# Output projection of a two-layer kernel: tiles transposed once for both of their uses and two tiles later, and one Strassen product moved behind another

## The chip, the core and the metric

The kernel runs on one core of one Trainium2 chip. The metric is the device time of one execution in microseconds (us); the time before is the median of three runs. TensorE is called PE here (PEld is its weight load), VectorE is DVE, ScalarE is ACT, GpSimd is POOL, and SP is the engine whose queue issues nearly all transfers.

## What is computed

A residual stack of two layers on `x` of shape 2 x 1024 x 512. Only the seam between the layers matters here:

```
xn = layernorm(x);  s = attn0(xn) @ Wo;  g = silu(ffn0(xn))
x  = x + s * g                       # the "join": output projection, gate, residual
xn = layernorm(x)                    # 2048 x 512, input of layer 1
s  = linear_recurrence(xn)           # works along time, wants xn with features on partitions
g  = silu(gelu_mlp(xn))              # 512 -> 4096 -> 512, 4-bit weights with scales
x  = x + s * g
```

Layer 1 uses the transposed `xn` twice. The recurrence reads it from DRAM (`xd`, 512 features x 1024 times for each batch); the MLP reads it from SBUF (`xq`), where the features are split into quarters for a Strassen product of 7 instead of 8 block products.

## The kernel before, in words

The rows are cut into 16 tiles of 128, in the order chunk by chunk and within a chunk batch 0, then batch 1 (L154): tile 14 is the last of batch 0 and tile 15 the last of batch 1. All matmuls are fp32; the profile counts two records for each.

**Join (class `Join`, L140).** `product` (L199) adds up 16 matmuls of 128x512 for a tile, one for each head, or 8 where half of the sum was made earlier and lies in DRAM (`pd`: tiles 4, 5, 7, 8, 10, 11, 12, 13). `rest` (L235) is what follows on DVE: add the earlier half (L231), multiply by the gate (L232), add the residual (L224) and write the sum to `x1d` for the end of the kernel (L225), statistics (L219 to L221), a power on POOL (L238) and the normalization (L239), which leaves `xn` in the buffer of the gate, `jg`. `jx` is the buffer of `x`. Products 0 to 2 are made within the last stage of layer 0; `run` (L245) makes products 3 to 15.

**Turn (L277).** For each tile PE transposes `xn` twice, four 128x128 pieces each time: once with the features in their order, for `xd` (ACT copies the PSUM tile into the now free `jx`, one DMA writes it out, L280), and once with even and odd features apart (`step=2`, a strided read), for `xq` (DVE copies, L121). After every second chunk four DVE instructions form the sums of the Strassen quarters (L286 to L289). Tile i is turned right after product i+1. PSUM has three banks for products and two for transposes, and a turn takes both.

**What sets the order.** In `run` the scheduler of the framework orders each engine's instructions at build time, by readiness, so unpacking of the first MLP weights (`hi`, `pk`, `w_g`, `w_u`, `w_d`) is mixed in between on DVE and POOL. In the second layer the order is written out by hand (class `Ordered`, L124). SP's queue is first in, first out: a DMA that waits holds up all behind it. `load_xg` (L188) loads `x` and gate of tile n into one of three buffers (`j_t` has one, `j_t2` two), once the tile three earlier has been turned and written; it is called two tiles ahead. `load_o` (L174) does so for the attention output `jo`, also with three buffers.

**Last tiles.** Tile 14 is turned halfway through product 15 (L260 to L262). Tile 15 is turned in the second layer: `run` returns its `turn`, and `last_turn` (L1582) runs it after five products of the first Strassen group, since that group works on batch 0 alone.

**Second layer.** `four` (L1394) makes the seven products of a weight block: `first` and so on to `seventh`, of two matmuls each, into three PSUM banks a, b, c. The products in bank a accumulate there and ACT takes copies in between; bank c is opened by `third` (P5 of the scheme) and added to by `sixth` (P3), which must wait until DVE has read the bank for `fourth`. The loop at L1594 runs gate (f=0), then up (f=1) for each group and batch. At the very first group and batch (n=0) the order is that of L1610: first, third, second, fifth, fourth, last turn, sixth; the gate's seventh comes in the second slot of the up half.

Of the kernel before, what the change touches and what calls it, by code (L numbers as in the profile page):

```python
# [22 lines left out]
P = 128  # L23
B, T, D = 2, 1024, 512
NT = B * T
KC = D // P
NTT = NT // P
# [36 lines left out]
def done(steps):  # L64
    for _ in steps:
        pass
# [39 lines left out]
def transposed(nc, psp, tag, dst, src, ident, engine, step=1):  # L106


    pt = psp.tile([P, KC, P], F32, tag=tag, name="ptr")
    for j in range(KC):  # L110
        if step == 1:
            s = src[:, j * P : (j + 1) * P]
        else:
            s = src.rearrange("p (kc q par) -> p kc par q", kc=2, par=2)[:, j // 2, j % 2, :]
        nc.tensor.transpose(pt[:, j, :], s, ident)
    if len(dst.shape) == 4:
        pt = pt.rearrange("p (a b) t -> p a b t", b=dst.shape[2])
    if engine == "scalar":
        nc.scalar.copy(dst, pt)
    else:  # L120
        nc.vector.tensor_copy(dst, pt)  # L121


class Ordered:  # L124
# [15 lines left out]
class Join:  # L140
# [47 lines left out]
    def load_xg(self):  # L188
        n = len(self.xg)
        c, b = self.order[n]  # L190
        ti = b * NC + c
        tp = self.tp[n % 3 > 0]
        xt = tp.tile([P, D], F32, tag="x", name=f"jx_{ti}")
        self.tc.nc.sync.dma_start(xt, self.a["x"][ti * P : (ti + 1) * P, :])
        g = tp.tile([P, D], F32, tag="g", name=f"jg_{ti}")
        self.tc.nc.sync.dma_start(g, self.gd[ti * P : (ti + 1) * P, :])
        self.xg.append((xt, g))
# [47 lines left out]
    def run(self, xd, xq, xp):  # L245

        nc, tc = self.tc.nc, self.tc
        with self.ctx as ctx:
            ps_o, ps_t = (
                ctx.enter_context(tc.tile_pool(name=n, bufs=bufs, space=PSUM, reuse_waits="tile"))  # L250
                for n, bufs in (("j_pso", 3), ("j_pst", 2))
            )
            late = None
            for i in range(NTT):
                if i >= self.made:
                    for _ in range(min(i + 3, NTT) - len(self.o)):
                        self.load_o()
                    product = self.product(ps_o, "pso", nc.tensor.matmul)
                    if i == NTT - 1:
                        done(itertools.islice(product, H // 2))  # L260
                        late(nc, ps_t, "pst", self.xg[i - 1][0].rearrange("p (k t) -> p k t", k=KC))
                    done(product)  # L262
                    g = self.xg[i][1]
                    if i == NTT - 1:
                        g = xp.tile([P, D], F32, name="xn_last")
                    for step in self.rest(g):
                        step()
                if late is not None and (i < NTT - 1 or i < self.made - 1):
                    late(nc, ps_t, "pst", self.xg[i - 1][0].rearrange("p (k t) -> p k t", k=KC))
                if late is not None:  # L270
                    for _ in range(min(i + 3, NTT) - len(self.xg)):
                        self.load_xg()
                g = g if i == NTT - 1 else self.xg[i][1]
                late = functools.partial(self.turn, xd, xq, *self.order[i], g)
        return late

    def turn(self, xd, xq, c, b, g, nc, psp, tag, xt):  # L277
        ident = self.cst[:, C_ID, :]
        transposed(nc, psp, tag, xt, g, ident, "scalar")
        nc.sync.dma_start(xd[b].rearrange("k p t -> p k t")[:, :, c * P : (c + 1) * P], xt)  # L280
        h, cols = c % 2, slice(c // 2 * P, (c // 2 + 1) * P)
        quarters = xq[b][:, 0:4].rearrange("p (kc h) par t -> p h kc par t", h=2)[:, h, :, :, cols]
        transposed(nc, psp, tag, quarters, g, ident, "vector", step=2)
        if h:
            b11, b12, b21, b22, t1, t2, t4 = (xq[b][:, q, :, cols] for q in range(7))
            nc.vector.tensor_tensor(t1, b12, b11, ALU.subtract)  # L286
            nc.vector.tensor_tensor(t2, b22, t1, ALU.subtract)
            nc.vector.tensor_tensor(t4, b21, t2, ALU.subtract)
            nc.vector.tensor_tensor(b12, b22, b12, ALU.subtract)  # L289
# [3 lines left out]
def first_layer(ctx, tc, a, cst, minus_half, keep, xnT, od, gd, pd, then):  # L293
# [471 lines left out]
    def within(hg, c, store):  # L765
# [25 lines left out]
        for s in range(NS):  # L791
            turn(pk[:, s, :], k[:, s, :])
# [88 lines left out]
    def finish(hg, c):  # L881
# [42 lines left out]
        for s in range(NS):  # L924
            turn(pot[:, s, :], on[:, s, :])
# [283 lines left out]
def second_layer(ctx, tc, a, cst, x1d, xd, xq, out, late):  # L1209
# [18 lines left out]
    nc = tc.nc  # L1228
# [13 lines left out]
    ident = cst[:, C_ID, :]  # L1242
# [75 lines left out]
    def group_weights(g, w):  # L1318

        g_, u_ = packed("g", g), packed("u", g)  # L1320
        yield
        wg, steps = quartered("g", g, *g_)
        yield from steps
        d_ = packed("d", g)
        wu, steps = quartered("u", g, *u_)
        yield from steps
        wd, steps = halved(g, *d_)
        yield from steps
        w += wg, wu, wd
# [163 lines left out]
    def down(g, b, wd):  # L1493

        left = inters[g, b]
        for i, j, n in (
            (A22, T4, 3), (A11, B11, 0), (A12, B21, 1), (S3, T3, 6), (S1, T1, 4), (S2, T2, 5), (S4, B22, 2)
        ):
            for half in range(2):
                po = ps_o.tile([P, 2, 256], F32, tag="pso", name=f"po_{g}_{b}_{n}_{half}")  # L1500
                for t in range(2):
                    c = (2 * half + t) * P
                    PE.matmul(
                        po[:, t, :], lhsT=left[i][:, c : c + P], rhs=wd[:, j, :], start=True, stop=True
                    )
                dst = acc[b][:, n, half]
                if g == 0:
                    DVE.tensor_copy(dst, po)
                else:
                    DVE.tensor_tensor(dst, dst, po, ALU.add)  # L1510
                yield

    def together(b):


        P1, P2, P3, P4, P5, P6, P7 = range(7)
        for dst, x, y in (
            (P6, P1, P6), (P1, P1, P2), (P7, P6, P7), (P4, P7, P4), (P7, P7, P5), (P5, P6, P5), (P3, P5, P3)
        ):
            for half in range(2):  # L1520
                DVE.tensor_tensor(acc[b][:, dst, half], acc[b][:, x, half], acc[b][:, y, half], ALU.add)
                yield
# [6 lines left out]
    def load_last():  # L1529
        for b, h, i in itertools.islice(ahead, 1):  # L1530
            ti = b * NC + 2 * i + h
            pool, *tags = next(rooms)
            y, x1 = (pool.tile([P, D], F32, tag=t, name=f"l{t}_{ti}") for t in tags)
            nc.sync.dma_start(y, yd[ti * P : (ti + 1) * P, :])
            nc.sync.dma_start(x1, x1d[ti])
            at_last[ti] = y, x1
# [51 lines left out]
    for n in range(2 * NG):  # L1588
        g, b = n // 2, n % 2
        if b == 0:  # L1590
            done(steps)
            wg, wu, wd = weights
            if g < NG - 1:
                weights = []  # L1594
                steps = group_weights(g + 1, weights)
        if n == 2 * NG - 2:
            for _ in range(4):
                load_last()
        if g == NG - 1:
            tog = together(b)  # L1600
        active = n - 1 in starts
        lasts = none
        if n == 2 * NG - 1:
            lasts = down_last(0, wd)
        for f, products in enumerate(up_and_gate(g, b, wg, wu)):
            for s in range(7):
                slot = 7 * f + s
                if n == f == 0:

                    (products[:1] + products[2:3] + products[1:2] + products[4:5] + products[3:4]  # L1610
                     + (last_turn, products[5]))[s]()
                elif s == 1:
                    before()
                else:
                    products[s - (s > 0)]()
                next(downs, None)
                if slot < 10:
                    next(lasts, None)
                if slot not in (0, 2, 4) or not active:
                    next(steps, None)  # L1620
                for _ in range(1 + (slot < 3) if g == NG - 1 else 0):
                    next(tog, None)
                if slot == 7 and n in starts:
                    recurring = recur(*starts[n])
                if slot not in (5, 8, 9):
                    next(recurring, None)
            before = products[6]
        done(downs)
        downs = down(g, b, wd) if g < NG - 1 else none
# [105 lines left out]
```

## Time and profile before

| | us |
|---|---|
| median of 3 runs (3189.05 to 3189.89) | 3189.33 |
| the profiled execution, its own time | 3191.48 |
| its span, first to last instruction | 3188.9 |
| outside the span in that execution | 2.58 |
| PE busy in the span | 3148.8 (99%) |
| DVE / ACT / POOL busy | 2147.2 / 1251.4 / 832.4 |
| join loop, first turn to first product of layer 1 | 1842.59 to 1984.16 |
| layer 1, steady part, PE without a gap | 2010 to 3150 |

How to read it: times in the trace count from the span's start. A timeline row gives start, duration, engine, line, output<-input and, in brackets, the idle time of the engine before it with what ended it. A row "x8" merges eight records. Matmuls are pipelined, so the duration of one record is longer than its share of the engine's time; the distance from the start of one row to the start of the next is what the work took. The granted TensorE clock was 1.00 in every window from 1842.5 to 3150.

### The profile page before, as it was taken

The numbers are of one execution on the slowest core, as the hardware profiler recorded it, in microseconds if no ns is written. First come the engines' busy times: TensorE is split into PE (matmuls) and PEld (weight loads), VectorE is DVE, ScalarE is ACT, GpSimd is POOL, SyncE is SP. The second block draws the span as 40 slices with busy tenths as digits, with TensorE's granted clock in tenths as the row PEclk, the third lists the DMA queues.
The fourth block names the chain that finished last, engine by engine and source line by source line (L and its number), as shares of the span: only waits on it lengthen the run. The fifth ranks groups of instructions, "written<-read, shape, count | busy, mean of one in ns | idle before, by whom it ended". The sixth has DMA issues, their size and how long they took to land.

```text
span 3188.9 us, 38235 instructions
## 1 busy us (share of the span) xinstructions
PE 3148.8 (99%) x12454; PEld 1950.8 (61%) x12454; DVE 2147.2 (67%) x4294; ACT 1251.4 (39%) x2269; POOL 832.4 (26%) x1210
## 2 busy tenths in 40 slices
PE   8999999999999999999999999999999999999998
PEld 6576756666666666666666644555555555555554
DVE  4557678786877878675554454677777666776676
ACT  3466555555555555434333200222222222322223
POOL 2000123222322222222222210332333333333222
PEclk9999999999999999999999999999999999999999
DMA  6244344444444443443334465010001000110014
GB/s 183 64 119 113 112 125 115 115 129 126 119 111 132 135 125 109 111 128 100 87 84 142 117 194 156 30 34 27 27 27 40 27 27 27 34 33 27 27 37 132
DMA packets 499494, 287.40 MB, mean 90 GB/s; under 512 B 207328, under 2 KB 440544, under 8 KB 499296
## 3 DMA queue, kind: packets, MB, share of 16 engines
q1 hardware_dynamic: 490432, 268.97, 29.9%
q0 software_dynamic: 6560, 11.80, 1.3%
q10 hardware_dynamic: 2304, 4.20, 0.4%
q8 instruction: 99, 1.62, 0.2%
q14 instruction: 99, 0.81, 0.1%
HBM read 183.90 MB, written 88.34 MB: 85 GB/s over the span
## 4 chain that ended last, share of the span: by engine, by line
PE 76%; DVE 5%; issue 2%; ACT 1%; DMA 1%; SPq 1%; POOL 0%; DVEq 0%; ACTq 0%; POOLq 0%
PE po L132 15%; PE pua L132 7%; PE pga L132 7%; PE pgate L132 6%; PE pwq L132 5%; PE pwv L132 5%; PE pwk L132 4%; PE zw L132 4%; PE pgc L132 3%; PE puc L132 3%; PE jpo L211 3%; PE pub L132 2%; PE pgb L132 2%; PE pr L132 2%; PE pks L132 1%
## 5 line engine op out<-in xcount | busy, mean ns | idle before, releaser
L132 DVE TENSOR_TENSOR acc<-acc,po 128x512 f32<-128x512 f32 x408 | 277.9, 681 | 208.7 <-PE po L132 207.9
L132 PEld LDWEIGHTS po<-w_d,i 128*128 128x128 f32 x1024 | 194.5, 190 | 142.6 <-issue 111.2
L132 PE MATMUL po<-w_d,i 128*128 128x256 f32 (+1 forms) x1024 | 275.4, 392 | 0.0
L132 PE MATMUL pgate<-xnT,wg 128*128 128x512 f32 x512 | 245.7, 593 | 0.0
L132 PE MATMUL pwq<-xnT,wq 128*128 128x512 f32 x512 | 245.1, 593 | 0.0
L132 PE MATMUL pwv<-xnT,wv 128*128 128x512 f32 x512 | 243.0, 594 | 1.8 <-ACT gate L132 1.8
L132 PE MATMUL pua<-xq,w_u 128*128 128x512 f32 x512 | 240.6, 592 | 0.0
L132 PE MATMUL pga<-xq,w_g 128*128 128x512 f32 x512 | 240.6, 592 | 0.0
L132 PE MATMUL pwk<-xnT,wk 128*128 128x512 f32 x512 | 237.6, 596 | 1.5 <-ACT ka L132 1.5
L132 ACT COPY g<-pga 128x512 f32<-128x512 f32 x96 | 56.2, 585 | 447.2 <-PE pga L132 432.8
L132 DVE SCALAR_TENSOR_TENSOR v<-prewv,cw,v 128x512 f32<-128x512 f32 x192 | 165.9, 865 | 63.4 <-ACT v L132 53.3
L132 PEld LDWEIGHTS po<-w_d,s 128*128 128x128 f32 x720 | 136.8, 190 | 95.4 <-issue 77.0
L132 ACT COPY w<-zw 128x128 f32<-128x128 f32 x192 | 50.6, 264 | 362.0 <-PE zw L132 362.0
L132 DVE TENSOR_TENSOR rr<-rr,zw 128x128 f32<-128x128 f32 x192 | 54.6, 284 | 199.2 <-PE zw L132 195.2
L132 PE MATMUL po<-w_d,s 128*128 128x256 f32 x720 | 184.8, 379 | 0.0
L132 ACT ACT_TABLE_LOAD x133 | 170.6, 1283 | 17.9 <-PE pr L132 11.3
L132 POOL TENSOR_TENSOR rs<-rs,minus_half 128x4 f32<-128x4 f32 x64 | 64.5, 1007 | 429.9 <-DVE rs L132 403.8
L132 POOL TENSOR_TENSOR ot<-ot,gate 128x512 f32<-128x512 f32 x64 | 85.9, 1343 | 343.4 <-ACT ot L132 313.7
L132 DVE SCALAR_TENSOR_TENSOR ka<-prewk,cw,ka 128x512 f32<-128x512 f32 x192 | 150.4, 785 | 34.9 <-ACT ka L132 23.2
L132 PEld LDWEIGHTS zw<-rr,ground 128*128 128x128 f32 x512 | 97.0, 191 | 124.5 <-issue 102.4
L132 DVE SCALAR_TENSOR_TENSOR q<-prewq,cw,q 128x512 f32<-128x512 f32 x192 | 159.8, 833 | 15.0 <-POOL eg L132 6.3
L132 PEld LDWEIGHTS zw<-w,ground 128*128 128x128 f32 x768 | 111.3, 192 | 65.6 <-issue 55.2
(248 smaller groups left out, 6661.6 us busy)
## 6 DMA issues: line engine op xcount, KB each, us to landing
e<-gr SPq DMA_DIRECT2D x64, 256.0 KB, 3.9
de<-e SPq DMA_DIRECT2D x64, 256.0 KB, 3.0
dk<-ka SPq DMA_DIRECT2D x32, 512.0 KB, 2.8
kb<-dk SPq DMA_DIRECT2D x64, 256.0 KB, 3.5
eb<-de SPq DMA_DIRECT2D x64, 256.0 KB, 3.0
eg<-egr SPq DMA_DIRECT2D x64, 256.0 KB, 3.9
od<-ot SPq DMA_DIRECT2D x64, 256.0 KB, 2.1
wt<-w SPq DMA_DIRECT2D x768, 16.0 KB, 2.0
```

The costliest lines, as they stand in the source:

```text
L132: i = getattr(self.engine, name)(*args, **kw)
L211: matmul(po, lhsT=ot[:, h, :], rhs=self.wo[h], start=(h == h0), stop=(h == H - 1))
```

## The change

Six edits, all in the seam:

1. `turn` transposes a tile once, in the split order. DVE copies the PSUM tile to `xq` as before, and ACT copies the same PSUM tile for `xd`. Since its rows now are in the order even, odd, the write to `xd` becomes two DMAs of 128 KB, one for each half of the features.
2. Tile i is turned after product i+2 instead of i+1 (the list `late` holds two tiles).
3. At tile 15, tile 13 is turned ahead of its product and tile 14 in its middle.
4. `x` and gate have four buffers instead of three (new pool `j_t3`); the loads are issued from the turn, four tiles ahead of the tile turned, with one extra at the first product.
5. `transposed` returns its PSUM tile.
6. In layer 1 at n=0, the gate's `sixth` (P3) is held and issued after the up half's `first` (P1).

```diff
-        tp = self.tp[n % 3 > 0]
+        tp = self.tp[(0, 1, 1, 2)[n % 4]]
...
+            self.tp.append(self.pool("j_t3", 1))
+            first = self.made
+            late = []
+            def turn():
+                i, step = late.pop(0)
+                step(nc, ps_t, "pst", self.xg[i][0].rearrange("p (k t) -> p k t", k=KC))
+                if len(self.xg) < min(i + 5, NTT):
+                    self.load_xg()
             for i in range(NTT):
+                if i == first:
+                    self.load_xg()
...
                     if i == NTT - 1:
+                        turn()
                         done(itertools.islice(product, H // 2))
-                        late(nc, ps_t, "pst", self.xg[i - 1][0].rearrange("p (k t) -> p k t", k=KC))
+                        turn()
...
-                if late is not None and (i < NTT - 1 or i < self.made - 1):
-                    late(nc, ps_t, "pst", self.xg[i - 1][0].rearrange("p (k t) -> p k t", k=KC))
-                if late is not None:
-                    for _ in range(min(i + 3, NTT) - len(self.xg)):
-                        self.load_xg()
+                if len(late) > 1:
+                    turn()
...
     def turn(self, xd, xq, c, b, g, nc, psp, tag, xt):
-        transposed(nc, psp, tag, xt, g, ident, "scalar")
-        nc.sync.dma_start(xd[b].rearrange("k p t -> p k t")[:, :, c * P : (c + 1) * P], xt)
...
-        transposed(nc, psp, tag, quarters, g, ident, "vector", step=2)
+        pt = transposed(nc, psp, tag, quarters, g, ident, "vector", step=2)
+        nc.scalar.copy(xt, pt)
+        for kc in range(2):
+            nc.sync.dma_start(
+                xd[b].rearrange("k p t -> (k p) t")[256 * kc : 256 * kc + 256, c * P : (c + 1) * P]
+                .rearrange("(p par) t -> p par t", par=2),
+                xt[:, 2 * kc : 2 * kc + 2],
+            )
...
-                     + (last_turn, products[5]))[s]()
+                     + (last_turn, lambda: None))[s]()
+                    held = products[5]
                 elif s == 1:
+                    if n == 0:
+                        held()
                     before()
```

The built order of the changed kernel differs from that of the kernel before in the seam alone. On PE the join's turns are rows of four transposes instead of eight, and the up half's P1 stands ahead of the gate's P3. On DVE and POOL the unpacking of the first down weights, `w_d`, with the two instructions that follow it (`hi_g`, `pk_g`), has moved from beside tile 14 to behind the normalization of tile 15 (DVE) and behind the last power (POOL), and the first of them waits for a DMA queue's semaphore, that of the `x1d` write of tile 15. ACT's copies for `xd` wait for DVE's copy of the same PSUM tile. On SP the loads for tile 3 no longer stand behind a write to `xd`, `pk_g` and `sc_g` come one `x` load earlier, and every write to `xd` is two entries.

More of the change, by code (lines that the diff above doesn't have):

```diff
@@ L115, in transposed @@
         nc.tensor.transpose(pt[:, j, :], s, ident)
-    if len(dst.shape) == 4:
-        pt = pt.rearrange("p (a b) t -> p a b t", b=dst.shape[2])
+    src = pt.rearrange("p (a b) t -> p a b t", b=dst.shape[2]) if len(dst.shape) == 4 else pt
     if engine == "scalar":
-        nc.scalar.copy(dst, pt)
+        nc.scalar.copy(dst, src)
     else:
-        nc.vector.tensor_copy(dst, pt)
+        nc.vector.tensor_copy(dst, src)
+    return pt
 class Ordered:
@@ L252, in run @@
             )
-            late = None
+            self.tp.append(self.pool("j_t3", 1))
[6 more added lines that the diff above has]
+                    self.load_xg()
             for i in range(NTT):
+                if i == first:
+                    self.load_xg()
                 if i >= self.made:
@@ L267, in run @@
                         step()
-                if late is not None and (i < NTT - 1 or i < self.made - 1):
-                    late(nc, ps_t, "pst", self.xg[i - 1][0].rearrange("p (k t) -> p k t", k=KC))
-                if late is not None:
-                    for _ in range(min(i + 3, NTT) - len(self.xg)):
-                        self.load_xg()
+                if len(late) > 1:
+                    turn()
                 g = g if i == NTT - 1 else self.xg[i][1]
-                late = functools.partial(self.turn, xd, xq, *self.order[i], g)
-        return late
+                late.append((i, functools.partial(self.turn, xd, xq, *self.order[i], g)))
+        return late[0][1]
     def turn(self, xd, xq, c, b, g, nc, psp, tag, xt):
         ident = self.cst[:, C_ID, :]
-        transposed(nc, psp, tag, xt, g, ident, "scalar")
-        nc.sync.dma_start(xd[b].rearrange("k p t -> p k t")[:, :, c * P : (c + 1) * P], xt)
         h, cols = c % 2, slice(c // 2 * P, (c // 2 + 1) * P)
         quarters = xq[b][:, 0:4].rearrange("p (kc h) par t -> p h kc par t", h=2)[:, h, :, :, cols]
-        transposed(nc, psp, tag, quarters, g, ident, "vector", step=2)
+        pt = transposed(nc, psp, tag, quarters, g, ident, "vector", step=2)
[6 more added lines that the diff above has]
+            )
         if h:
```

## The prediction

> **What bounds the kernel.** I read the busy table and its slices, then the busy times by stage, then PE's timeline through the seam, since the change touches nothing else. By stage (columns: window, length, busy time of PE, PEld, DVE, ACT, POOL with counts, granted clock, DMA share, GB/s):
>
> ```profile
> 1842.50:1984.20 141.70, 138.11 (x412) 67.60 (x411) 74.70 (x168) 11.14 (x19) 20.18 (x26) 1.00 0.62 189
> 1984.20:2010.00 25.80, 25.22 (x66) 11.52 (x65) 16.19 (x30) 7.64 (x12) 3.99 (x5) 1.00 0.23 72
> 2010.00:2300.00 290.00, 290.00 (x906) 170.41 (x905) 200.25 (x294) 77.34 (x113) 96.38 (x105) 1.00 0.09 29
> ```
>
> PE is never idle from 2010 to 3150, so whatever PE gains or loses in the seam moves the end by as much. In the join loop it is idle for 3.6 of 141.7 us: PE sets the pace there too, with two gaps. Its timeline:
>
> ```profile
> 1867.08 1.10 PE L115 MATMUL ptr<-cst,jg 128*128 128x128 f32 x8 [0.90 <-DVE sp_e L100]
> 1868.02 7.03 PE L211 MATMUL jpo<-wo,jo 128*128 128x512 f32 x16
> 1877.74 1.10 PE L115 MATMUL ptr<-cst,jg 128*128 128x128 f32 x8 [2.69 <-DVE jg L239]
> 1878.68 13.90 PE L211 MATMUL jpo<-wo,jo 128*128 128x512 f32 x32
> 1892.42 1.07 PE L115 MATMUL ptr<-cst,jg 128*128 128x128 f32 x8
> 1893.33 7.03 PE L211 MATMUL jpo<-wo,jo 128*128 128x512 f32 x16
> ...
> 1976.35 1.11 PE L115 MATMUL ptr<-cst,jg 128*128 128x128 f32 x8
> 1977.29 7.03 PE L211 MATMUL jpo<-wo,jo 128*128 128x512 f32 x16
> 1984.16 1.88 PE L132 MATMUL pga<-xq,w_g 128*128 128x512 f32 x4
> ...
> 1992.75 1.07 PE L132 MATMUL ptr<-cst,xn_last 128*128 128x128 f32 x8
> 1994.40 1.96 PE L132 MATMUL pgc<-xq,w_g 128*128 128x512 f32 x4 [0.58 <-DVE g L132]
> 1996.19 1.88 PE L132 MATMUL pua<-xq,w_u 128*128 128x512 f32 x4
> 1997.91 1.88 PE L132 MATMUL pga<-xq,w_g 128*128 128x512 f32 x4
> ```
>
> Read distances between starts: eight transposes take 1892.42 to 1893.33, 0.91 us; half a product (16 records) 6.87; a whole one 1878.68 to 1892.42, 13.74. The brackets are PE's waits: two turns wait for a late normalization, and the gate's P3 (`pgc`) waits for DVE.
>
> **Half the transposes go.** Four of eight fall away in each of 16 turns. What is a transpose worth? [...] The starts say otherwise: eight fit into 0.91 us, because they are pipelined, and the four of `pot`, in plain order, take 1842.15 to 1842.59, 0.44 us. I use the starts. The plain four go, the strided four stay: 0.91 - 0.44 = 0.47. Once, at 1845.66, four strided ones stood alone and took 0.56; they had just got their PSUM bank back, which the lag removes. I take 0.47, with 0.56 as the other end. Gain 15 x 0.44 = 6.6 us in the loop, 0.44 in the last turn.
>
> **The waits in the loop go.** Products 3 to 15 are five whole and eight half ones: 5 x 13.74 + 8 x 6.87 = 123.66. With 15 turns of 0.91 (13.65) that is 137.31; the loop took 1984.16 - 1842.59 = 141.57. The other 4.26 are the two waits (0.90 and 2.69), a slow restart behind each, and 0.14 at tile 14. With the lag a turn needs the normalization of the tile before last. A normalization was done 6 to 12 us after its product (the long ones where DVE, busy for 18.99 of 20 us from 1860 to 1880, also unpacks weights), and now has at least 14.7 us (two half products and two turns). Counting DVE's new order: `pk_g` comes some 3 us earlier on SP, the unpacking of `w_g` ends at about 1856.6 where product 3 ends, tile 3 is normalized at about 1862 and turned at 1871.5, tile 4 at about 1871 and turned at 1885.7. Even with `pk_g` as late as before (1855.7) 6 us are left at tile 3. What is late next is nothing on DVE. Tile 14 keeps one half product and a turn (7.8 us); its power on POOL stood behind `w_d` sums until 1975.07, which are moved away, and the pair of turns ahead of product 15 adds one DVE copy (0.6): ready at about 5 us. So the loop becomes 123.66 + 15 x 0.47 = 130.71, **10.86 less**.
>
> **Costs beside it, taken as nothing.** Each `xd` write is two DMAs: one SP entry more, 0.38 us, 16 times. ACT's copy now waits for DVE's. [...] Before, the two copies went their own ways, on two banks: ACT copied at 1893.10, DVE at 1894.01. Serialized, a turn's two copies need 0.69 + 0.58 and occupy the bank to about 2.1 us after the turn starts. On PE's path, 0.58 x 16 would be 9.3 us and eat most of the gain; but with two banks and a turn each 7.3 us no transpose waits for it, and I take 0. The write to `xd` then issues at 2.9 us, lands in 2.8 (median; at most 5.2), and the `x` load behind it on SP lands about 4.3 later (median from 1880 to 1945): 10.3 us after the turn. DVE wants that `x` 14.7 us after it. The cover is 4.4 us; beyond that the lag gives 9 us more before PE waits.
>
> Behind these waits on SP stand gate, `jo` and `x1d`; `jo` is loaded two products ahead, as before. The fourth buffer frees tile 3's load. The same bytes move in less time: about 25.1 MB from 1842.5 to 1960 (214 GB/s) become about 235 GB/s, below the 251 of 1860 to 1880 at a DMA share of 0.82.
>
> **The head of layer 1.** From 1992.75 the order was eight transposes, P3, up's P1, the gate's seventh at 1997.91: 5.16 us. Now four transposes (0.47), P1 (1.72), P3 (1.72): 3.91. P3 starts at 1994.94 by the old clock; DVE's read of bank c (1993.56 + 0.69) is over. **1.25 less.** What can be late next is up's `third` (bank c) at about 2000.1: it needs DVE's add after P3, which DVE does behind the turn's copy and sums and two `w_g` steps, by my count at 1999.4. ACT's copy for up's fourth product ends at about 2001.2, wanted at 2001.8.
>
> Here lies the one new wait. `w_d` now stands on DVE ahead of the gate's adds and waits until tile 15's `x1d` write (issued 1985.87) has landed; queued behind it are the adds for which ACT and then P3 wait. By the trace's 3.0 median it lands at 1988.9, and the 3.55 us of DVE work up to the add of 1993.56 fits if it lands by 1990.0. At the longest landing of the trace, 7.6, that is 3.5 us late; at the least, 2.2, free. Beside POOL's `w_d` sums a DVE step also stretched (`pk_g` 1.09 us at 1972.75 against 0.69). I take 0.3 lost.
>
> **Sum.** 10.86 + 1.25 - 0.3 = 11.8 us. The profiled execution took 3191.48 (span 3188.9); it becomes 3179.7. It lies 2.15 above the median of the runs, and I move the median by the same: 3189.33 - 11.8 = **3177.5 us**.
>
> **Rivals.**
>
> - *Only the transposes count; the waits come back elsewhere* (DVE from 1855 to 1885 stays behind, or P3's wait moves to `third`). For: DVE is nearly full there. Against: 6 us and more of new slack. Then the gain is 7.0 to 8.3: about 3181.7.
> - *The `w_d` wait bites:* the `x1d` write lands late behind other transfers. Price up to 3.5: 3181.0. Against: the DMA share is 0.28 from 1985 to 2000.
> - *Slower: the ring of `x` buffers becomes the bound.* Copy after copy, two writes, then a load behind both on one in-order queue. It decides when the round trip passes 14.7 + 9.5 = 24 us, against my 10.3; each further us is lost once in each four tiles. To end 6.4 us above the old time it must lose 18 us over three rounds: a trip of 30 us, 3196 us in all. For: the engines' share reaches 0.82. Against: same bytes, same pieces of 512 B.
>
> That the change doesn't do what it says is excluded: the built order shows 64 transposes less on PE.
>
> **Chances.** 0.2% (6.4 us, about what a measurement of this kernel can tell from no change) puts the line for faster at 3182.9. The forecast 0.75 (3175.5 to 3179.5); waits come back 0.10, of which a third lies above the line; `w_d` 0.07; slower 0.05; unknown small waits 0.03. Faster 0.87, same 0.08, slower 0.05. The range runs from 3175.5 (no loss, restarts smaller) to 3183 (strided four at 0.56, 1.4 us, with the late write).
>
> **What would show it.** PE's rows in the loop: turns of x4 with 0.47 between starts, no bracket; first `pga` about 10.9 earlier, at 1973.3; no bracket on `pgc` or `puc`; DVE waiting for PE at the end of each product. Wrong would be: brackets at the turns of tiles 3 to 5 (rival one), at `pga` to `puc` with DVE behind `w_d` (two), at `jpo` or turns late in the loop, ended by `x` loads (three).

## The result and the profile after

| | before | after |
|---|---|---|
| median of 6 runs each, us | 3189.61 (3189.01 to 3192.11) | 3176.10 (3174.20 to 3178.39) |
| profiled execution, its own time | 3191.48 | 3174.2 |
| its span | 3188.9 | 3172.4 |
| first turn to first gate product (loop) | 141.57 | 130.63 |
| last turn to the gate's seventh (head) | 5.16 | 3.91 |

The ratio is 0.9959 with a 95% interval of 0.9949 to 0.9969: 13.5 us faster, with 9.9 to 16.3 us inside the interval. 3177.5 was forecast.

Busy times by stage of the changed kernel; the columns are those of the same view before (window, length, busy time of PE, PEld, DVE, ACT, POOL with counts, granted clock, DMA share, GB/s):

```profile
1838.40:1969.10 130.70, 130.70 (x351) 61.92 (x350) 71.65 (x164) 11.25 (x19) 15.76 (x22) 1.00 0.66 205
1969.10:2010.00 40.90, 40.90 (x114) 20.95 (x113) 32.35 (x51) 10.59 (x18) 16.74 (x17) 1.00 0.18 58
2010.00:2300.00 290.00, 290.00 (x904) 170.02 (x903) 201.82 (x295) 79.38 (x115) 95.61 (x104) 1.00 0.09 28
```

PE's busy time now equals the window's length in the loop and in the head, where 3.6 and 0.6 us of idle time stood before. Its timeline through the same places:

```profile
1852.65 0.63 PE L115 MATMUL ptr<-cst,jg 128*128 128x128 f32 x4
1853.12 7.03 PE L211 MATMUL jpo<-wo,jo 128*128 128x512 f32 x16
1859.99 0.63 PE L115 MATMUL ptr<-cst,jg 128*128 128x128 f32 x4
...
1953.92 1.11 PE L115 MATMUL ptr<-cst,jg 128*128 128x128 f32 x8
...
1969.07 1.88 PE L132 MATMUL pga<-xq,w_g 128*128 128x512 f32 x4
...
1977.65 0.63 PE L132 MATMUL ptr<-cst,xn_last 128*128 128x128 f32 x4
1978.12 1.88 PE L132 MATMUL pua<-xq,w_u 128*128 128x512 f32 x4
1979.84 1.88 PE L132 MATMUL pgc<-xq,w_g 128*128 128x512 f32 x4
1981.56 1.88 PE L132 MATMUL pga<-xq,w_g 128*128 128x512 f32 x4
```

No row carries a bracket any more. A transpose leaves one record, so x4 is a turn of four. It takes 0.47 from start to start (1852.65 to 1853.12), as forecast; the x8 row is the pair of turns ahead of product 15. The loop lost 10.94 us and the head 1.25: **12.2 us in the seam**. The two spans differ by 16.5; 4.15 of that lies ahead of the first turn (1842.59 and 1838.44), where both kernels have the same order of instructions on every engine. There the profiled execution of before had the granted clock at a half from 1241.4 for 3.4 us and from 1330.2 for 6.8 us, the one after nowhere. That part is not the change: in the fourteen profiles of this document the first turn starts anywhere from 1838.05 to 1844.10, and the earliest of all is a second execution of before. What the seam gains does reach the end: from the gate's seventh to the last instruction all fourteen take 1190.0 to 1191.2 us.

### The profile page after: what moved, and what is told of

The parts are those of the page before. It is cut to its first block, busy times and chain, and to the rows that moved or that the text cites. A ratio compares the mean times of both kernels' runs of the same rounds, so it can differ in the third digit from the quotient of the medians.

```text
span 3172.4 us, 38119 instructions
## 1 busy us (share of the span) xinstructions
PE 3138.0 (99%) x12390; PEld 1941.4 (61%) x12390; DVE 2148.2 (68%) x4294; ACT 1251.4 (39%) x2269; POOL 833.4 (26%) x1210
## 4 chain that ended last, share of the span: by engine, by line
PE 89%; DVE 5%; ACT 2%; issue 2%; DMA 1%; SPq 1%; POOL 0%; DVEq 0%; ACTq 0%; POOLq 0%
PE po L132 18%; PE pua L132 7%; PE pga L132 7%; PE pwk L132 6%; PE pgate L132 6%; PE pwv L132 5%; PE pwq L132 5%; PE jpo L211 4%; PE zw L132 4%; PE puc L132 3%; PE pgc L132 3%; PE pu L132 3%; PE pg L132 3%; PE pr L132 2%; PE pub L132 2%; PE pgb L132 2%
```

## Experiments

All distances are from the starts of PE's rows; "loop" and "head" are those of the table above. Medians are given beside those of the kernel before in the same comparison; their 95% intervals reach 2 to 4 us to either side, so steps of one or two us are read from the distances alone.

| kernel | loop | head | median | before beside it |
|---|---|---|---|---|
| turn alone (once_only) | 137.91 | 5.16 | 3186.75 | 3190.96 |
| lag alone (lag_only) | 137.36 | 5.16 | 3184.25 | 3189.37 |
| P3 alone (p3_only) | 143.21 | 4.34 | 3187.60 | 3189.37 |
| changed, lag undone (lag_one) | 136.76 | 3.90 | 3183.38 | 3189.08 |
| changed, turn undone (turned_twice) | 137.59 | 4.35 | 3182.65 | 3189.08 |
| changed, P3 undone (p3_back) | 130.62 | 5.16 | 3176.52 | 3189.08 |
| changed, three buffers | 130.63 | 3.90 | 3175.61 | 3189.08 |
| changed, one transpose bank | 130.75 | 3.90 | 3176.69 | 3190.96 |
| changed, stress | 130.63 | 3.89 | 3176.83 | 3190.96 |
| changed, x1d in pieces | 130.63 | 5.85 | 3179.81 | 3190.96 |
| changed, again | 130.63 | 3.90 | 3175.49 | 3189.37 |
| before, again | 142.57 | 5.16 | 3189.13 | 3189.37 |

**The lag undone.**

```diff
                     if i == NTT - 1:
-                        turn()
                         done(itertools.islice(product, H // 2))
                         turn()
...
-                if len(late) > 1:
+                if late and (i < NTT - 1 or i < self.made - 1):
                     turn()
```

> The changed kernel, but each tile is turned one product after its own, as before; transposed once, four buffers and the held P3 stay. If the lag is what took the waits away, DVE's late normalizations of tiles 3 and 4 are PE's waits again: PE comes to these turns 0.44 us a turn earlier than in the kernel before, so the waits there (0.90 and 2.69, with their restarts 4.1) grow by about that; the loop from the first turn to the first gate product is 135.0 to 136.0 instead of 130.63 us, and the kernel is 4.5 us slower than the changed one (3180.6). If instead the fourth buffer and the earlier loads had taken the waits away, the loop stays within 1 us of 130.6.

The loop took 136.76, 6.13 more. PE's timeline at tiles 3 and 4, with its wait in brackets:

```profile
1865.41 0.71 PE L115 MATMUL ptr<-cst,jg 128*128 128x128 f32 x4 [0.25 <-DVE sp_e L98]
...
1876.95 1.10 PE L115 MATMUL ptr<-cst,jg 128*128 128x128 f32 x4 [3.96 <-DVE sp_e L100]
1877.85 14.98 PE L211 MATMUL jpo<-wo,jo 128*128 128x512 f32 x32
```

The waits are back at the same two tiles, 4.21 together (`sp_e` is only the last DVE instruction before the one that was waited for, the normalization). So it is the lag, and not the fourth buffer or the earlier loads, that takes them. The 0.8 us more than expected stand in the last two rows: the turn took 0.90 to the next start instead of 0.47, and the product lasted 14.98 instead of 13.90. The windows of this kernel behind the wait show why:

```profile
1877.30:1880.70 3.40, 3.40 (x9) 1.79 (x8) 3.40 (x8) 0.35 (x1) 3.06 (x4) 0.60 1.07 362
1880.70:1892.60 11.90, 11.90 (x29) 5.27 (x28) 4.11 (x10) 0.24 (x1) 1.38 (x2) 1.00 0.47 151
```

The granted clock is 0.60 right behind the wait and 1.00 again after it: some 1.5 us lost on top of the wait. More of this below.

**The turn undone.** The whole `turn` of before, in the changed kernel.

```diff
-        pt = transposed(nc, psp, tag, quarters, g, ident, "vector", step=2)
-        nc.scalar.copy(xt, pt)
-        for kc in range(2):
-            nc.sync.dma_start(
...
+        transposed(nc, psp, tag, xt, g, ident, "scalar")
+        nc.sync.dma_start(xd[b].rearrange("k p t -> p k t")[:, :, c * P : (c + 1) * P], xt)
+        transposed(nc, psp, tag, quarters, g, ident, "vector", step=2)
```

> The changed kernel with the old turn: two times four transposes into two PSUM banks, two independent copies, one write to xd; lag, four buffers and the held P3 stay. If four transposes are worth their distance between starts, each of 15 turns in the loop is 0.44 longer and the last one too: loop 137.2 instead of 130.63, head 4.35 instead of 3.91, in all 7.0 us slower (3183.1). [...] If the serialized copies or the doubled writes had cost anything, the difference is smaller than 7.0, since they go here.

Loop 137.59, head 4.35: 6.96 and 0.44 more, 7.4 us. Two turns of its timeline and the pair at product 15:

```profile
1853.38 1.08 PE L115 MATMUL ptr<-cst,jg 128*128 128x128 f32 x8
...
1861.16 1.08 PE L115 MATMUL ptr<-cst,jg 128*128 128x128 f32 x8
...
1961.39 1.30 PE L115 MATMUL ptr<-cst,jg 128*128 128x128 f32 x8
1962.53 6.17 PE L211 MATMUL jpo<-wo,jo 128*128 128x512 f32 x14
```

7.78 from turn to turn, less 6.87 for the half product, leaves 0.91: the turn of before, without any wait. The pitch of the starts is the price, not the 279 ns of a record (the median of the 120 in before), which would have given 17.9 for 64 of them. The 0.4 above the expected 7.0 is mostly the turn at 1961.39, which took 1.14 instead of 0.91. The turn ahead of it had just taken both banks; that this is the reason is not shown.

**P3 in its old place.**

```diff
-                     + (last_turn, lambda: None))[s]()
-                    held = products[5]
+                     + (last_turn, products[5]))[s]()
                 elif s == 1:
-                    if n == 0:
-                        held()
                     before()
```

> The changed kernel with P3 of the first four in its old place, directly behind the last turn and ahead of up's P1. P3 waits there for DVE's read of bank c; in the kernel before it started 1.65 us after the turn. If DVE's pace is what counts, it starts there again whatever the turn takes: turn to gate's seventh 1.65 + 3 x 1.72 less one = 5.1 instead of 3.91, 1.2 us slower. If the reordering was worth only the 0.74 of bracket and restart that the profile before shows, it is 0.7. If the wait has only moved, nothing.

```profile
1978.40 0.63 PE L132 MATMUL ptr<-cst,xn_last 128*128 128x128 f32 x4
1980.05 1.96 PE L132 MATMUL pgc<-xq,w_g 128*128 128x512 f32 x4 [1.02 <-DVE g L132]
```

P3 starts 1.65 us after the turn, to the hundredth where it started before with eight transposes; its bracket has grown from 0.58 to 1.02 by just what the turn saved. Head 5.16. Here DVE sets the pace, and without the move the last turn's saving would have been worth nothing.

**Three buffers.**

```diff
-        tp = self.tp[(0, 1, 1, 2)[n % 4]]
+        tp = self.tp[n % 3 > 0]
...
-            self.tp.append(self.pool("j_t3", 1))
...
-                if len(self.xg) < min(i + 5, NTT):
+                if len(self.xg) < min(i + 4, NTT):
...
-                if i == first:
-                    self.load_xg()
```

> The changed kernel with three buffers for x and gate instead of four: the load of tile i+3 stands behind the turn of tile i, directly ahead of product i+3, and nothing is loaded ahead at the first product. It tests the ring of buffers. By my count the gate and x arrive about 10 us after the turn and tile i+3 is turned three products later, at least 22 us: DVE starts later with each tile but PE does not wait: loop 130.6 to 131.5, the kernel within 1 us of the changed one. If the round trip is the bound that the third rival took it for, brackets on turns ended by DVE appear and the loop grows by 3 us or more.

Loop 130.63, no bracket: the fourth buffer is worth nothing to PE. But little was left. DVE's timeline in this kernel, and the turn of tile 14 on PE:

```profile
1946.57 0.69 DVE L224 TENSOR_TENSOR jx<-jg,jx 128x512 f32<-128x512 f32 x1 [3.49 <-DMA jx<-in_x]
...
1961.24 0.94 DVE L239 TENSOR_SCALAR jg<-jx,ln_mv,ln_rs 128x512 f32<-128x512 f32 x1 [1.12 <-POOL ln_rs L238]
```

```profile
1962.51 0.63 PE L115 MATMUL ptr<-cst,jg 128*128 128x128 f32 x4
```

DVE waited for `x` four times, 7.5 us in all, where it never did with four buffers; the deeper lag hid it. In this built order `w_d` also stands beside tile 14 again, and POOL's power came late: the normalization ended 0.3 us before PE turned the tile, against 2.8 in the changed kernel.

**The turn alone**, in the kernel before (new `turn` and `transposed`, nothing else).

```diff
-        transposed(nc, psp, tag, xt, g, ident, "scalar")
-        nc.sync.dma_start(xd[b].rearrange("k p t -> p k t")[:, :, c * P : (c + 1) * P], xt)
...
-        transposed(nc, psp, tag, quarters, g, ident, "vector", step=2)
+        pt = transposed(nc, psp, tag, quarters, g, ident, "vector", step=2)
+        nc.scalar.copy(xt, pt)
+        for kc in range(2):
...
```

> The kernel before with the new turn alone (four transposes, shared bank, two writes); lag of one, three buffers and P3's place as before. The theory is that DVE sets PE's pace at tiles 3 and 4 and at P3, so what the turns save ahead of these points is eaten by longer waits there: 15 x 0.44 = 6.6 minus three turns up to tile 4 (1.3): loop 136.2 to 137 instead of 141.57, and nothing in the head (P3 still 1.65 after the turn, 5.16 in all). 4.6 to 5.3 us faster than the kernel before: 3184. If the saving counts in full: loop 134.97, head 4.7, 7.0 faster. If a wait near 4 us brings the granted clock to a half as in the run with a lag of one, 1.5 us less gain.

Loop 137.91: 3.66 gained instead of the 6.6 that the transposes are worth, and 0.9 less than the least expected. Waits of PE from its timeline:

```profile
1867.53 0.72 PE L115 MATMUL ptr<-cst,jg 128*128 128x128 f32 x4 [1.24 <-DVE sp_e L100]
1878.29 1.10 PE L115 MATMUL ptr<-cst,jg 128*128 128x128 f32 x4 [3.17 <-DVE jg L239]
...
1974.59 0.72 PE L115 MATMUL ptr<-cst,jg 128*128 128x128 f32 x4 [0.65 <-DVE jg L239]
...
1992.25 1.96 PE L132 MATMUL pgc<-xq,w_g 128*128 128x512 f32 x4 [1.02 <-DVE g L132]
```

Each wait is longer than before (0.90, 2.69, at tile 14 a slow restart of 0.14, 0.58), and the product behind the second was slow again (turn to turn 15.75 instead of 14.20). So of the 3 us that are missing about half are longer waits, since a faster PE only reaches the same normalization sooner, and 1.55 are the slow clock behind the longest of them, which the profile of before did not have.

**The lag alone**, in the kernel before (old turn, three buffers, old place of P3).

```diff
-                if late is not None and (i < NTT - 1 or i < self.made - 1):
-                    late(nc, ps_t, "pst", self.xg[i - 1][0].rearrange("p (k t) -> p k t", k=KC))
...
+                if len(late) > 1:
+                    turn()
```

> The kernel before with the lag of two tiles alone: old turn with eight transposes, three buffers, P3 in its old place. The run with the turn alone gained 3.66 us in the loop and nothing in the head, since DVE's waits ate the rest. If lag and turn hang together, the lag alone takes the waits (4.26, less 0.28 for the pair ahead of product 15, as the run with two times four transposes had it): loop 137.6, head 5.16, 4.0 us less than before in the trace; both alone then sum to 7.6, and the two together gave 10.9. If they simply add, the lag alone is worth 10.94 - 3.66 = 7.3.

Loop 137.36, 4.2 less, head 5.16. So turn alone (3.66) and lag alone (4.2) sum to 7.9, both together gave 10.94: the missing 3 us are the longer waits and the slow clock that eat into the turn's saving as long as the lag is one.

**P3 alone**, in the kernel before.

```diff
-                     + (last_turn, products[5]))[s]()
+                     + (last_turn, lambda: None))[s]()
+                    held = products[5]
                 elif s == 1:
+                    if n == 0:
+                        held()
                     before()
```

> The kernel before with P3 of the first four behind up's P1 alone. With eight transposes in the last turn P3 waited 0.58 (with its restart 0.81 against the pitch of 1.72): head 4.35 instead of 5.16, 0.8 us faster, loop as before at 141.57. If the move is worth the whole 1.25 that the changed kernel has in its head, 3.91. It is also the fourth profile with a lag of one: the three so far all showed the clock at a half at about 1242 us, none of the seven with a lag of two did, though the order of the instructions up to 1838 is the same; if that is chance, it need not be here.

Head 4.34, 0.82 less; the median cannot tell so small a step from nothing (ratio 0.9995, interval 0.9987 to 1.0003). But the loop, untouched by this edit, took 143.21 instead of 141.57. The control below shows why.

**One bank for the transposes.**

```diff
-                for n, bufs in (("j_pso", 3), ("j_pst", 2))
+                for n, bufs in (("j_pso", 3), ("j_pst", 1))
```

> The changed kernel with one PSUM bank for transposes instead of two. It prices the two copies that now stand behind one another on one bank. A bank is in use until about 2.1 us after the turn starts; turns are 7.3 us or more apart, so single turns cost nothing; only the pair ahead of product 15 (tiles 12 and 13) stands back to back, where the second turn must wait for both copies of the first: 2.1 - 0.47 = 1.6 us, loop 132.3 instead of 130.63, a bracket ended by ACT there and nowhere else. If the serialized copies are on PE's path in general, each turn shows a bracket and the loop grows by up to 0.58 for each (8.7).

Loop 130.75, 0.12 more. The built order put four records of product 15 between the two turns of the pair, so they no longer stood back to back:

```profile
1958.20 0.63 PE L115 MATMUL ptr<-cst,jg 128*128 128x128 f32 x4
1958.67 1.88 PE L211 MATMUL jpo<-wo,jo 128*128 128x512 f32 x4
1960.41 0.74 PE L115 MATMUL ptr<-cst,jg 128*128 128x128 f32 x4
```

The expected 1.6 us did not come. ACT's copy of the first turn ended at 1960.36, 2.16 us after the turn began, and the next transposes followed at 1960.41. So the occupation of a bank was counted rightly (2.1), and in this order even one bank hides the serialized copies; the price for two turns truly back to back stayed untested.

**Stress.** Three buffers (edited as above), four writes to `xd` instead of two, and the copy on ACT three times over.

```diff
-        nc.scalar.copy(xt, pt)
-        for kc in range(2):
+        for _ in range(3):
+            nc.scalar.copy(xt, pt)
+        for kc in range(KC):
```

> The changed kernel with everything against it that the third rival needs: three buffers, each write to xd in four DMAs of 64 KB instead of two of 128, and ACT making its copy three times over. Together some 1.4 (two more copies) + 0.8 (two more queue entries) us more in each round trip of a buffer, which starts one product later as well. With 9 us and more of lag behind it nothing of that reaches PE: loop 130.6 to 131.2. If the cover is thinner than my count, brackets ended by DVE at turns, 1 to 10 us.

Loop 130.63. The `x` load behind the turn at 1882.43 was issued 9.0 us after it, against 7.6 in the changed kernel (1881.53, 1889.17): the trip did grow by 1.4, and nothing of it reached PE. Here too the normalization of tile 14 ended only 0.3 us before its turn.

**The x1d write of tile 15 in eight pieces.**

```diff
-                    nc.sync.dma_start(self.x1d[ti], xt)
+                    k = 8 if i == NTT - 1 else 1
+                    for r in range(k):
+                        p = slice(r * P // k, (r + 1) * P // k)
+                        nc.sync.dma_start(self.x1d[ti][p], xt[p])
```

> The changed kernel with the x1d write of tile 15 in eight DMAs of 16 rows instead of one: the last lands some 7 x 0.38 = 2.7 us later. It tests the wait of w_d on DVE, which in the changed kernel cost nothing (the write landed at about 1972.8, w_d started at 1973.2 straight behind the normalization). Now w_d should start some 2.3 us later; of that the waits of DVE's adds for ACT (1.05) and P3's own slack (0.68) take 1 to 1.7 us. 0.6 to 1.3 us are lost in the head: 4.5 to 5.2 instead of 3.91. If the wait can't bite at all (w_d goes later without holding up the adds), 3.91 stays; if it bites at once, 6.2.

DVE's timeline, first in this kernel (where the normalization is L242), then in the changed one:

```profile
1974.50 0.55 DVE L242 TENSOR_SCALAR xn_last<-jx,ln_mv,ln_rs 128x512 f32<-128x512 f32 x1 [0.73 <-POOL ln_rs L241]
1977.71 1.29 DVE L132 SCALAR_TENSOR_TENSOR w_d<-pk_d,sc_d 128x512 f32<-128x512 f16 x2 [2.67 <-DMA x1d<-jx]
...
1982.77 0.69 DVE L132 TENSOR_TENSOR g<-g,pgc 128x512 f32<-128x512 f32 x1 [0.83 <-ACT g L132]
```

```profile
1972.61 0.55 DVE L239 TENSOR_SCALAR xn_last<-jx,ln_mv,ln_rs 128x512 f32<-128x512 f32 x1 [0.73 <-POOL ln_rs L238]
1973.19 1.29 DVE L132 SCALAR_TENSOR_TENSOR w_d<-pk_d,sc_d 128x512 f32<-128x512 f16 x2
...
1978.47 0.69 DVE L132 TENSOR_TENSOR g<-g,pgc 128x512 f32<-128x512 f32 x1 [1.05 <-ACT g L132]
```

With the eight writes `w_d` waits 2.67; without, the write (issued 1970.77, 2.0 to its landing) is done before the normalization is. PE's P3 then waited 1.72 for the add and the head took 5.85: 1.94 more. Of 2.67 only 0.73 was covered. I had counted ACT's 1.05 as cover as well; it is almost none, since ACT itself waits for an add that stands behind `w_d` and moves with it (its bracket only fell to 0.83). Mechanism right, cover about half of what I took. The second rival's wait is real, and it decides from 0.7 us on; in the changed kernel it isn't there.

**Controls.** Both kernels once more, unaltered.

> The changed kernel once more, unaltered, as a measure of what two executions differ by. The seam's distances, 130.63 and 3.91, should be the same to 0.05 us. What is left between the medians (13.5) and the seam (12.2) should show as a difference ahead of the first turn, from stretches at half clock near 1242 and 1330 us: a first turn at 1838.4 to 1842.7 here too if these are chance.

> The kernel before once more, unaltered: ratio 1.000 within 0.0008. Loop 141.57 and head 5.16 to 0.3 us (the waits at tiles 3 and 4 hang on DVE and a transfer). If the clock at a half near 1242 us belongs to the executions and not to the kernel, it may be absent here; if it is there again, four of four or five of five with a lag of one show it.

The changed kernel repeats to 0.01 us. The kernel before doesn't: its loop took 142.57. PE's timeline at tiles 3 and 4 in this second execution of before:

```profile
1861.87 1.10 PE L115 MATMUL ptr<-cst,jg 128*128 128x128 f32 x8 [0.21 <-DVE sp_e L100]
...
1872.54 1.36 PE L115 MATMUL ptr<-cst,jg 128*128 128x128 f32 x8 [2.69 <-DVE jg L239]
1873.69 15.35 PE L211 MATMUL jpo<-wo,jo 128*128 128x512 f32 x32
```

The wait is 2.69 as in the first, but the product behind it lasts 15.35 where it was 13.90. The window of 3.4 us behind the wait, in this execution and then in the first one:

```profile
1872.50:1875.90 3.40, 3.37 (x11) 2.20 (x12) 3.30 (x7) 0.59 (x1) 0.00 (x0) 0.60 0.65 156
```

```profile
1877.70:1881.10 3.40, 3.36 (x14) 2.12 (x15) 3.30 (x7) 0.59 (x1) 0.00 (x0) 1.00 0.72 173
```

The same stretch of work runs at a clock of 0.60 in one execution and of 1.00 in the other. The count of PE's records in it (11 and 14) says the same. The slow clock cost 1.66 us (16.34 from turn to turn instead of 14.68), and the wait at tile 3 was 0.69 shorter: together the 1.0 by which the loop is longer.

## Why the prediction was right

- **Transposes, 0.91 to 0.47.** Right to the hundredth, and the choice of starts over durations was the one that mattered: turned_twice put 7.4 us on what the durations would have made 17.9 (eight records of 279 ns overlap so far that they fit into 0.91). The 0.56 taken as the other end for strided pieces never appeared in the changed kernel; turns behind a wait took 0.55 (lag_one, once_only), so it goes with the restart and not with the stride: strided turns without a wait took 0.47.
- **Waits in the loop, 4.26.** Right, and right in its cause: lag_one brought them back, three buffers did not, and lag_only took them away without the new turn. The loop was forecast at 130.71 and took 130.63. The two counted normalizations were done 21.2 and 30.6 us after the first turn, 1.8 and 2.2 later than counted, so tile 3 had 7.7 us left instead of 9.5; the margin took the miss. Tile 14, counted to be ready 5 us into its 7.8, had the 2.8 us left that this makes.
- **The parts are not independent.** The sum charged 6.6 to the turn and 4.26 to the lag. Alone they give 3.66 and 4.2. The sum was right because both were there; the split holds only with the lag in place, which the prediction did not say.
- **Costs taken as nothing.** In all 15 turns ACT's copy began after DVE's had ended; the two hold a bank for 2.1 us as counted and cost nothing, against the 9.3 they would have cost on PE's path. A write to `xd` took SP about 0.6 an entry, not 0.38 (two at 1884.61 in 1.23), and the round trip was about 12 us (1881.53 to 1889.17, and 4.5 median to the landing), not 10.3. Two landing times of the prediction mix the reads of a tensor with its writes: the writes of before alone have a median of 3.3 (`xd`) and 3.6 (`x1d`), not 2.8 and 3.0. The DMA rate over the loop rose from 189 to 205 GB/s, by 8%, as the same bytes in less time make it, and the 235 came: 234 over the 106.7 us behind the first turn, the stretch that ended at 1960 shortened by the gain. The trip of 12 us stayed within the cover of 14.7. How an entry of SP that waits holds up the next shows in before: ACT's copy for a write to `xd` had ended at 1893.69, but the write was issued at 1895.48, behind the `x1d` write of 1894.12, which had waited for DVE's add until 1894.09.
- **Head, 1.25.** Right: 3.91. The up half's third product (`puc`) started at 1984.99, DVE's add for it had ended at 1984.34, so the 0.65 us that are left are the 0.7 counted.
- **`w_d`, 0.3 lost.** It cost nothing; the write landed 3.7 us after the first gate product by the trace (1970.77 + 2.0, 1969.07) and 4.7 by my count. That and the 0.1 of the loop are the difference between 12.2 and 11.8.
- **From 12.2 to the 13.5 of the medians.** The interval of the ratio (9.9 to 16.3 us) holds 11.8 and 12.2 as well. What the profiles show beside that: I took the 141.57 of one profiled execution for the loop of every run. Three profiles now hold that loop (the two of before, and p3_only, which doesn't touch it): 141.57, 142.57 and 143.21, since in two of them the clock fell behind the 2.69 wait. Their mean is 142.5, which makes the loop's gain 11.8 and the seam's 13.1. Three profiles are few, and the clock also fell ahead of the seam, near 1241 or 1330 us, in ten of the fourteen profiles; the last 0.4 us are within the noise. That the one profile at hand had no fall in the loop was chance; with one, the same sum would have come out 1.7 us larger.

The first rival fell with the empty brackets; the third did not cost PE anything even with three buffers and stress, though there with 0.3 us to spare. No version here beats the changed kernel beyond the spread of its runs; three buffers take the same time with less memory and less margin.

## What to carry to other kernels

Take the price of a pipelined instruction from the distance between starts (0.47 us for four transposes whose records last 0.28 each), and check with the parts one by one whether the engine that you speed up has the pace: work saved ahead of a wait only lengthens that wait, so the deeper lag was what let the halved transposes count. Cover is only what doesn't hang on the delayed instruction itself: an idle bracket further down the same chain moves along and hides almost nothing (ACT's 1.05 shrank by 0.22 under a delay of 2.67). And a wait can cost more than its bracket, by the clock behind it (here 1.5 to 1.7 us more, in four of five executions); compare more than one profile before a sum is made to the tenth.

## What the runs showed of the hardware

The granted TensorE clock fell to 0.50 behind waits of PE, and not every time. At tile 4 of the join it fell in four of five executions that had a wait there (2.69 twice of three times, 3.17, 3.96), and each cost 1.5 to 1.7 us more. Near 1241 us a wait of 1.7 was followed by it in five of the fourteen profiles, and near 1330 a wait of 2.8 to 4.0 in nine of them (and a wait of 3.1 to 3.5 was not in the other five), with the same order of instructions in all.

In each of the five profiles with at least two stretches at half clock ahead of the kernel's end (before, lag_one, once_only, lag_only, p3_only), the starts lie a multiple of 3.413 us apart. In before they are 1241.40, 1330.15 and 3183.58, the later two 26 and 569 times 3.413 behind the first; in lag_one 1241.73, 1330.47 and 1876.61, 26 and 186 times. In once_only, by the clocks of windows of 3.4 us, they are about 423.98, 1243.18, 1331.92 and 1878.05: 240, 26 and 160 times from one to the next. Ahead of the kernel's end a stretch lasted 3.4 or 6.8 us in all eleven profiles that had one. Where the starts lie relative to the work changes from one execution to the next: near 1241 the stretch began 1.54 us after the wait's end in before and 0.84 in lag_one. Windows cut at this spacing around the 2.69 wait at tile 4, in before_again and then in before:

```profile
1869.78:1873.20 3.42, 0.73 (x7) 0.70 (x7) 2.92 (x9) 0.00 (x1) 0.94 (x1) 1.00 0.94 292
1873.20:1876.61 3.41, 3.41 (x8) 1.84 (x8) 3.32 (x6) 0.58 (x1) 0.00 (x0) 0.50 0.64 159
```

```profile
1872.87:1876.28 3.41, 2.18 (x6) 0.63 (x4) 3.41 (x9) 0.00 (x0) 1.06 (x2) 1.00 1.00 312
1876.28:1879.70 3.42, 1.96 (x11) 1.51 (x12) 2.90 (x6) 0.59 (x1) 0.73 (x1) 1.00 0.73 219
```

In before_again the whole wait falls into one step of 3.41, and the next step runs at half clock; in before the steps cut the wait into 1.23 and 1.46, and nothing follows. The same cutting at the other places: in before the step ahead of 1241.40 had 1.68 us of PE's idle time and the step ahead of 1330.15 had 2.63. In after, with the steps counted back from its only stretch (3167.07, at the kernel's end), the wait of 1.68 near 1241 falls into 1.42 and 0.26 and the one of 3.52 near 1330 into 1.93 and 1.59, and the clock stayed at 1.00. So 1.68 in one step was followed by a fall and 1.93 in another was not: what decides is not shown.

A wait of 2.69 at tile 4 cost 2.69 in one of three executions and some 1.7 more in the other two.
